# Gated layers of a fused sequence kernel: feed-forward pieces spread over the four steps of a group, the next group's transposes two steps earlier, rotation sums emitted ahead of the softmax's normalisation

## The chip, the cores and the metric

The kernel runs on one core of a Trainium2 chip. The metric is device time in microseconds of one execution; lower is better. TensorE (PE in the profile, PEld for its weight loads) multiplies matrices into PSUM, VectorE (DVE) and ScalarE (ACT) take results out of PSUM and do elementwise work, GpSimd (POOL) works between buffers in SBUF, and SyncE (SP) issues the DMAs.

## What is computed

A sequence of 2 x 2048 tokens with 256 features goes through four blocks, each with a residual connection: a windowed attention layer with a feed-forward, two gated layers (DEPTH is 2), a gated attention unit, and a ternary linear layer. The change concerns the two gated layers alone. Cut to what matters:

```
def _layer(x, wqkv, qs, ksc, wo, lg, lb, w1, b1, w2, b2):
    h = shift_token(x)            # second half of the features comes from the token before
    q, k, v = split(h @ wqkv)     # 8 heads of 64
    q = l2norm(q) * qs
    k = l2norm(k) * ksc
    q, k = rotary_xpos(q, k)
    o = local_attention(q, k, v)  # a token sees itself and the 128 before it, softmax
    x = x + o @ wo
    h = shift_token(x)
    h = layernorm(h) * lg + lb
    a, g = split(h @ w1 + b1)     # 682 each
    h = a * gelu(g)
    x = x + h @ w2 + b2
    return x
```

## The kernel before

The 4096 tokens are 32 tiles of 128 (NT); four tiles make a group (GT = 4, NG = 8). The residual stream R stays in SBUF for the whole kernel. The kernel runs its blocks one after another; everything is in float32, where one matmul of the source shows as two in the profile.

The gated layers are a software pipeline over steps. A table `steps`, filled by `at(step, what, ...)`, says what a step does. With `s0` as the first step of a layer (the second layer begins GAP = 2 steps after the first layer's last tile), tile t is projected in step s0 + t, its scores are made in s0 + t + 1, its weights transposed in s0 + t + 2 and applied to the values in s0 + t + 3. So one step works on four tiles at once, called p (project), q (scores), a (weights) and o (values) in the loop.

The stages of a tile and their lines:

- `project` (L679): four matmuls of the source (two parts of the features, query and key), and two for the values in `project(2)`. ScalarE copies the result to `raw` (L689), squares it into `sq` (L690), copies the values (L686); GpSimd makes the sine products `u2` (L695, L698).
- `norms`: VectorE sums the squares (L710), GpSimd raises the sums to the power -1/2 (L711, L713), giving `rn`.
- `rotate_mul` and `rotate_add`: VectorE's cosine product (L718), the sum with the sine product (L722), and for the key the product with `rn` (L724). `to_features` transposes the result on TensorE (L731) and ScalarE copies it (L733).
- `scores`, in two halves: 32 small matmuls each (L748), mask and row maximum on VectorE (L757), the shift of the exponent (L764). `exponents` is four exps on ScalarE (L775). `normalise` is a reciprocal (L783) and four products (L786) on VectorE.
- `weights_to_keys` transposes a half of the softmax weights (L795, L803); the copies out of PSUM are L799 (ScalarE, first half), L797 (VectorE, second half) and L806 (ScalarE).
- `values` (L820, L832), copies L840 and L841, then `output`: four matmuls with wo (L847) and the sum into R on VectorE (L850).

The feed-forward works on a whole group and is cut into pieces. In the step `prepare`, DMAs fetch the shifted rows `sh` from R, VectorE makes the statistics (L881 to L883), GpSimd rs (L93, L95), VectorE normalises into `h` (L887); `to_features` transposes it (L117, ScalarE L122) and adds b2 to R on GpSimd (L895). Then six `hidden` pieces: four matmuls of the source with 512 columns (L908) for the first five, two (L917) for the sixth, which holds the last 42 features of both halves; gelu on ScalarE (L921) and the product with the other half on VectorE (L922), into one buffer `hh`. Then four `output` pieces, six matmuls each (L929), with a sum into R (L933). Each output piece reads all six parts of `hh`.

`begin` transposes the residual stream of a group before its first projection (L653, copies by ScalarE L654) and carries one column over from the group before (L649, GpSimd). `tables` loads the rotary tables of a group and multiplies them by a scale on GpSimd (L637).

A step has three places where feed-forward pieces stand between its other work, `fill[0]`, `fill[1]`, `fill[2]`. The loop emits a step in a fixed order; what matters of it is: values and scores(0); projection of query and key between exponents(0) and scores(1); norms, rotate_mul(0), project(2); exponents(1) and normalise(0); fill[0]; output; rotate_add(0); both halves of weights_to_keys; rotation of the key; normalise(1); fill[1]; the feed-forward's normalise; transposes of the query; fill[2]; transposes of the key; the feed-forward's to_features; begin.

A tile framework orders the instructions of each engine's queue from this program, with the emitted order as priority, so that a queue's order is near the emitted one but not the same. It also places buffers: all PSUM banks come from one pool of eight (`ps`), `za` and `zb` of `begin` have two buffers, `h`, `hT` and `hh` one.

Of the kernel before, what the change touches and what calls it, by code (L numbers as in the profile page):

```python
# [21 lines left out]
GT = 4  # L22
# [23 lines left out]
def kernel(ctx: ExitStack, tc: tile.TileContext, I: dict, out: bass.AP):  # L46
# [86 lines left out]
    def load_qkv(l):  # L133
        w = {}
        w["wqkv"] = T(wB, [P, KC, 3 * BIN], "wqkvB")
        load(w["wqkv"], I["L0_ffn_wqkv"][l].rearrange("(k p) n -> p k n", p=P))
        return w

    def load_wo(l):
        w = {}  # L140
        w["wo"] = T(wB, [P, BIN // P, D], "woB")
        load(w["wo"], I["L0_ffn_wo"][l].rearrange("(k p) n -> p k n", p=P))
        return w
# [33 lines left out]
    with ExitStack() as st_a:  # L177
# [284 lines left out]
        def at(step, what, *args):  # L462
            steps.setdefault(step, {}).setdefault(what, []).append(args)
# [5 lines left out]
        for g in range(NG):  # L469
            at(GT * g - 2, "load", g)  # L470
            at(GT * g - 1, "begin", g)
            s = GT * (g + 1) + 2
# [7 lines left out]
        groups, tiles, ffns, done = {0: first_group}, {}, {}, None  # L480
        for s in range(min(steps), max(steps) + 1):
            todo = steps.get(s, {})
            p = a = f = n = q = None
# [5 lines left out]
            if "project" in todo:  # L489
                (t,) = todo["project"][0]  # L490
                p = tiles[t] = TileA(t, groups[t // GT])
            if "scores" in todo:
                q = tiles[todo["scores"][0][0]]
            if "attend" in todo:
                a = tiles[todo["attend"][0][0]]
            fill = [lambda x=x: ffns[x[0]].output(x[1]) for x in todo.get("outputs", ())]
            fill += [lambda x=x: ffns[x[0]].hidden(x[1]) for x in todo.get("hidden", ())]
            fill = {0: [], 2: [fill[0:1], fill[1:], []], 4: [fill[0:2], fill[2:3], fill[3:4]]}[len(fill)]
            fill = fill or [[], [], []]
# [58 lines left out]
    def load_weights_c():  # L558
        load(uvw, uvT)
        load(uvb_r, bcast_rows(uvb[0 : 2 * CE], 2 * CE))  # L560

        hs = CS // 2
        load(uvw_sw[:, :, 0:hs], uvT[:, :, 2 * CE + hs : CUV])
        load(uvw_sw[:, :, hs:CS], uvT[:, :, 2 * CE : 2 * CE + hs])

        def column(src):
            return src.rearrange("(p o) -> p o", o=1)

        vectors = [uvb[2 * CE : CUV]]
        vectors += [I["L1_attn_gamma"][i] for i in range(2)] + [I["L1_attn_beta"][i] for i in range(2)]  # L570
        for i, v in enumerate(vectors):
            load(cvec[:, 0, i : i + 1], column(v))
            load(cvec[0:hs, 1, i : i + 1], column(v[hs:CS]))
            load(cvec[hs:CS, 1, i : i + 1], column(v[0:hs]))
        load(lnC[:, 0, :], I["L1_attn_ln_w"].rearrange("(k p) -> p k", p=P))
        load(lnC[:, 1, :], I["L1_attn_ln_b"].rearrange("(k p) -> p k", p=P))
        load(owC, I["o_wT"].rearrange("(k p) n -> p k n", p=P))
        load(obC, bcast_rows(I["L1_attn_o_b"], D))
        load(wD, I["ffn_wT"].rearrange("(k p) n -> p k n", p=P))
        load(bD, bcast_rows(I["L1_ffn_bias"], D))  # L580
        load(alpha, bcast_rows(I["L1_ffn_alpha"], 1))


    with ExitStack() as st_b:
# [47 lines left out]
        def load_tab(g, sv):  # L632

            tab = T(wb, [P, 4, GT, BHD], "tab")
            t0 = g % GPS * GT
            load(tab, I["rope_b"][:, :, t0 : t0 + GT, :])
            nc.gpsimd.tensor_mul(tab, tab, sv.unsqueeze(2).to_broadcast([P, 4, GT, BHD]))  # L637
            return tab

        def begin_b(g, zb_last):  # L640
            seq_start = g % GPS == 0
            Rg = R[:, g * GT : (g + 1) * GT, :]

            za = T(wb, [P, GN], "za")
            zb = T(wb, [P, GN + 1], "zb")
            if seq_start:
                nc.gpsimd.memset(zb[:, 0:1], 0.0)
            else:
                nc.gpsimd.tensor_copy(zb[:, 0:1], zb_last[:, GN : GN + 1])  # L649
            for k, dst in enumerate((za, zb[:, 1 : GN + 1])):  # L650
                pt = bank4()
                for tt in range(GT):
                    nc.tensor.transpose(pt[:, tt, :], Rg[:, tt, k * P : (k + 1) * P], ident)  # L653
                nc.scalar.copy(dst, pt.rearrange("p t c -> p (t c)"))  # L654
            return za, zb
# [287 lines left out]
        for l in range(BL):  # L943
            s0 = l * (NT + GAP)
            for t in range(NT):
                at(s0 + t, "project", l, t)
                at(s0 + t + 1, "scores", l, t)
                at(s0 + t + 2, "weights", l, t)
                at(s0 + t + 3, "values", l, t)
                if t % GT == 0:  # L950
                    at(s0 + t - 2, "tables", l, t // GT)
                    at(s0 + t - 1, "begin", l, t // GT)
            for g in range(NG):
                s = s0 + GT * (g + 1) + 3
                at(s, "prepare", l, g)
                for c in range(BNC):
                    at(s + 1 + c // 3, "hidden", l, g, c)
                for tt in range(GT):
                    at(s + 3 + tt // 2, "outputs", l, g, tt)
            at(s0 + NT - 1, "free_qkv", l)  # L960
            at(s0 + NT + 2, "free_wo", l)
            at(s0 + NT + 7, "free_ffn", l)
# [4 lines left out]
        groups, tiles, ffns = {}, {}, {}  # L967
        sh = None
        for s in range(min(steps), max(steps) + 1):
            todo = steps.get(s, {})  # L970
            p = a = q = o = None
            if "project" in todo:
                l, t = todo["project"][0]
                if l == BL - 1 and t == GT:
                    load_weights_c()
                p = tiles[l, t] = Tile(l, t, wts[l], tabs[l, t // GT], *groups[l, t // GT], tiles.get((l, t - 1)))
            if "scores" in todo:
                q = tiles[todo["scores"][0]]
            if "weights" in todo:
                a = tiles[todo["weights"][0]]  # L980
            if "values" in todo:
                o = tiles[todo["values"][0]]
            fill = [lambda x=x: ffns[x[0], x[1]].output(x[2]) for x in todo.get("outputs", ())]
            fill += [lambda x=x: ffns[x[0], x[1]].hidden(x[2]) for x in todo.get("hidden", ())]
            for l, g in todo.get("tables", ()):
                tabs[l, g] = load_tab(g, scales[l])
            if "prepare" in todo:
                l, g = todo["prepare"][0]
                f = ffns[l, g] = Ffn(l, g, wts[l])
                sh = f.shifted(sh)  # L990
            fill += [lambda: None] * (3 - len(fill))

            if o:
                o.values()
                o.prev = None
            if a:
                a.swap_values()
            if q:
                q.scores(0)
            if p:  # L1000
                p.project(0)
            if q:
                q.exponents(0)
            if p:
                p.project(1)
            if q:
                q.scores(1)
            if p:
                p.norms()
                p.rotate_mul(0)  # L1010
                p.project(2)
            if q:
                q.exponents(1)
                q.normalise(0)
            fill[0]()
            if o:
                o.output()
                tiles.pop((o.l, o.t - 1), None)
            if p:
                p.rotate_add(0)  # L1020
            if a:
                a.weights_to_keys(0)
                a.weights_to_keys(1)
            if p:
                p.rotate_mul(1)
                p.rotate_add(1)
            if q:
                q.normalise(1)
            fill[1]()
            if "prepare" in todo:  # L1030
                f.normalise()
            if p:
                p.to_features(0)
            fill[2]()
            if p:
                p.to_features(1)
            if "prepare" in todo:
                f.to_features()
            for l, g in todo.get("begin", ()):
                groups[l, g] = begin_b(g, groups[l, g - 1][1] if g else None)  # L1040
            for (l,) in todo.get("free_qkv", ()):
                if l + 1 < BL:
                    wts[l + 1] = load_qkv(l + 1)
            for (l,) in todo.get("free_wo", ()):
                if l + 1 < BL:
                    wts[l + 1].update(load_wo(l + 1))
            for (l,) in todo.get("free_ffn", ()):
                if l + 1 < BL:
                    wts[l + 1].update(load_ffn(l + 1))
# [303 lines left out]
```

## Time and profile before

| what | value |
|---|---|
| runs, us | 3016.64, 3003.9, 3003.57 |
| median, us | 3003.9 |
| profiled execution, us | 3012.32 |
| its span, first to last instruction, us | 3010.5 |
| mean granted TensorE clock | 0.959 |

The profile is one execution. Its page gives the busy time of every engine; a trace of it can be asked for a window, an engine or a line. In a timeline, a line is: start in us, duration in us, engine, source line, operation, what it writes and reads, shapes, how many were merged, and in brackets the idle time ahead of it with what is taken to have ended it. In sums by stage, a line is: window, its length, then for PE, PEld, DVE, ACT and POOL the busy time with the number of instructions, then the granted clock as a share of full speed, the DMA share and GB/s.

The costliest lines of the gated layers on TensorE, from the groups by line:

| line | what | instructions | busy, us |
|---|---|---|---|
| L908 | hidden pieces | 640 | 287.4 |
| L679 | projections, both parts | 768 | 411.7 |
| L929 | output pieces | 768 | 176.3 |
| L847 | attention output | 512 | 121.0 |
| L748 | scores | 4032 | 116.6 |

ScalarE loads a table of functions 28 times ahead of gelu (L921) and 28 times ahead of exp (L775) in these layers, 1283 ns each in the mean.

### The profile page before, as it was taken

What the parts mean: (1) busy time and instruction counts of PE and PEld (TensorE: products, weight loads), DVE (VectorE), ACT (ScalarE), POOL (GpSimd) and SP (SyncE); (2) the same over time, 40 slices, a digit from 0 to 9 for tenths busy, and PEclk for the clock granted to TensorE, in tenths of its full rate; (3) what the DMA queues carried; (4) which work ended last, traced back from release to release, by engine and by line L of the source; (5) the groups of instructions that cost most, each with busy time, mean ns of one, the idle gap of its engine ahead of it and who ended that gap; (6) DMA issues with size and microseconds to landing.
All of it is one profiled execution on the core that took longest, in us unless ns stands there. A gap on an engine that the chain in (4) does not pass through costs nothing. (4 is left out here: it accounts for less than half of the span.)

```text
span 3010.5 us, 50610 instructions
## 1 busy us (share of the span) xinstructions
PE 2727.0 (91%) x20146; PEld 1687.9 (56%) x20146; DVE 1703.0 (57%) x4457; ACT 1148.4 (38%) x2441; POOL 962.4 (32%) x935
## 2 busy tenths in 40 slices
PE   5788888896899999998989999999999999899998
PEld 3455556663566666665656666666544455444454
DVE  6766676634656566665666556665553334643333
ACT  2434443524555555554655555554230000210000
POOL 4443444324433333332344333342410012400001
PEclk8889999997899999999999999999999999999999
DMA  5000000002100100111111100101100000000000
GB/s 153 14 27 25 27 20 20 20 18 67 26 19 19 26 23 22 26 36 34 34 42 29 29 20 26 33 22 26 47 27 0 7 8 7 21 7 4 7 6 13
DMA packets 72764, 78.17 MB, mean 26 GB/s; under 512 B 18686, under 2 KB 57937, under 8 KB 72529
## 3 DMA queue, kind: packets, MB, share of 16 engines
q1 hardware_dynamic: 72528, 74.94, 8.9%
q8 instruction: 159, 2.61, 0.4%
q14 instruction: 77, 0.62, 0.1%
HBM read 42.50 MB, written 8.40 MB: 17 GB/s over the span
## 5 line engine op out<-in xcount | busy, mean ns | idle before, releaser
L1251 PE MATMUL ps<-V,s 128*128 128x512 f32 x1024 | 468.4, 593 | 3.2 <-DVE s L1183 3.2
L775 ACT ACTIVATE S<-S,shift,rn 128x192 f32<-128x192 f32 x512 | 274.3, 538 | 247.6 <-DVE shift L764 247.2
L1251 PEld LDWEIGHTS ps<-V,s 128*128 128x128 f32 x1024 | 190.6, 190 | 226.3 <-issue 220.4
L695 POOL TENSOR_TENSOR u<-raw,tab 128x256 f32<-128x256 f32 x128 | 124.0, 969 | 513.2 <-ACT raw L689 513.2
L908 PE MATMUL ps<-hT,w1B 128*128 128x512 f32 x640 | 287.4, 593 | 0.4 <-ACT hT L122 0.4
L679 PE MATMUL ps<-wqkvB,za 128*128 128x512 f32 x384 | 213.8, 639 | 5.9 <-ACT za L654 5.9
L1206 POOL TENSOR_SCALAR veC<-mvC 128x1 f32<-128x1 f32 x32 | 16.5, 517 | 601.1 <-DVE mvC L1204 601.1
L1179 DVE SCALAR_TENSOR_TENSOR s<-ps,strip 128x512 f32<-128x512 f32 x128 | 88.3, 690 | 206.9 <-PE ps L1173 206.9
L365 POOL TENSOR_TENSOR S<-S,mxA 128x1024 f32<-128x1024 f32 x64 | 121.2, 1894 | 259.2 <-DVE mxA L364 215.2
L679 PE MATMUL ps<-wqkvB,zb 128*128 128x512 f32 x384 | 197.9, 597 | 0.0
L713 POOL TENSOR_TENSOR rn<-ss,mhalf 128x16 f32<-128x16 f32 x64 | 195.5, 3055 | 5.2
L1194 ACT COPY oCT<-ps 128x512 f32<-128x512 f32 x32 | 18.7, 585 | 467.1 <-PE ps L1192 467.1
L908 PEld LDWEIGHTS ps<-hT,w1B 128*128 128x128 f32 x640 | 117.9, 190 | 131.0 <-issue 123.4
L929 PE MATMUL ps<-w2B,hh 128*128 128x256 f32 x768 | 176.3, 381 | 2.4 <-DVE top L757 2.4
L757 DVE CUSTOM_DVE_ANT_0 S<-ps,maskB 128x192 f32<-128x192 f32 x512 | 151.5, 350 | 22.9 <-PE ps L748 22.9
L731 PE MATMUL ps<-ident,u 128*128 128x128 f32 x512 | 80.2, 286 | 92.7 <-DVE rdB L783 57.5
L929 PEld LDWEIGHTS ps<-w2B,hh 128*128 128x128 f32 x768 | 143.8, 190 | 35.7 <-issue 11.5
L786 DVE TENSOR_SCALAR S<-S,rdB 128x192 f32<-128x192 f32 x512 | 159.2, 362 | 2.2
L718 DVE TENSOR_TENSOR u<-raw,tab 128x512 f32<-128x512 f32 x128 | 91.4, 715 | 113.3 <-ACT raw L689 109.7
L439 PE MATMUL ps<-hT,wf 128*128 128x512 f32 x256 | 131.9, 651 | 25.4 <-DVE oT L404 20.1
L722 DVE TENSOR_TENSOR u<-u,u 128x512 f32<-128x512 f32 x128 | 90.0, 703 | 89.6 <-POOL u L698 86.7
L731 PEld LDWEIGHTS ps<-ident,u 128*128 128x128 f32 x512 | 63.8, 147 | 129.7 <-issue 63.2
(210 smaller groups left out, 5566.2 us busy)
## 6 DMA issues: line engine op xcount, KB each, us to landing
vs<-v SPq DMA_DIRECT2D x128, 128.0 KB, 2.4
tab<-in_rope_b_dram SPq DMA_DIRECT2D x16, 512.0 KB, 3.8
xg<-in_L_attn_x_dram SPq DMA_DIRECT2D x8, 512.0 KB
xr<-in_L_attn_x_dram SPq DMA_DIRECT2D x8, 512.0 KB, 7.1
xs<-xr SPq DMA_DIRECT2D x8, 512.0 KB, 2.7
h<-xs SPq DMA_DIRECT2D x8, 512.0 KB, 3.6
rc<-in_rope_c_dram SPq DMA_DIRECT2D x8, 512.0 KB, 4.1
out_dram<-R SPq DMA_DIRECT2D x32, 128.0 KB, 1.7
```

The costliest lines, as they stand in the source:

```text
L365: nc.gpsimd.tensor_sub(Sh, Sh, mc.unsqueeze(2).to_broadcast([P, 2 * AG, P]))
L439: nc.tensor.matmul(pm, wf1[:, k, c * P : (c + 1) * P], self.hT[:, k, :], start=k == 0, stop=k == KC - 1)
L679: nc.tensor.matmul(pm, src[:, cols], self.w["wqkv"][:, k, part * BIN : (part + 1) * BIN], start=k == 0, stop=k == 1,)
L695: nc.gpsimd.tensor_mul(u2[:, :, 0:hd2], x[:, :, hd2:BHD], sin[:, :, 0:hd2].to_broadcast([P, BH, hd2]))
L713: nc.gpsimd.tensor_tensor(self.rn, ss, mhalf, ALU.pow)
L731: nc.tensor.transpose(pt[:, j, :], self.u1[part][:, 2 * j : 2 * j + 2, :], ident)
L757: nc.vector.tensor_tensor_reduce(S[:, e, jj, :], sc[e][:, jj * KW : (jj + 1) * KW], self.mask[:, jj, :], 1.0, -3.0e38, ALU.add, ALU.max, t ...
L775: nc.scalar.activation(S[:, e, jj, :], S[:, e, jj, :], AF.Exp, bias=self.shift[half][:, a : a + 1], scale=self.rn[:, head : head + 1], acc ...
L786: nc.vector.tensor_scalar_mul(S[:, e, jj, :], S[:, e, jj, :], rd[:, a : a + 1])
L908: nc.tensor.matmul(pm, w["w1"][:, k, half, c * P : (c + 1) * P], hT[:, k, :], start=k == 0, stop=k == KC - 1,)
L929: nc.tensor.matmul(pm[:, 0:D], hh[:, c, tt * P : (tt + 1) * P], self.w["w2"][:, c, :], start=c == 0, stop=c == BNC - 1,)
L1251: nc.tensor.matmul(acc[i], s2[:, i * P : (i + 1) * P], self.V[:, J, :], start=J == 0, stop=J == TPS - 1,)
```

## The change

Three things are moved; no operation is added or taken out.

1. The pieces. With s as the step that prepares a group, the six hidden pieces stood in s + 1 (three) and s + 2 (three), the outputs in s + 3 (two) and s + 4 (two), which is the next group's prepare step. Now there are two hidden pieces in each of s + 1, s + 2 and s + 3, one output in s + 3 after them, and three in s + 4. Hidden and output pieces share one list, `fill`, in the order in which `at` put them there. In s + 3 the order is hidden 4, hidden 5, output 0.
2. `begin` of a group moves from the step before the group's first tile, which is a prepare step in the run of a layer, to two steps earlier, which is s + 2.
3. In the loop, `rotate_add(0)` is emitted before `output` and no longer after it, and `normalise(0)` after the key's rotation and no longer before `fill[0]`; `fill[1]` is emitted before `normalise(1)`.

```diff
                 if t % GT == 0:
                     at(s0 + t - 2, "tables", l, t // GT)
-                    at(s0 + t - 1, "begin", l, t // GT)
+                    at(s0 + t - 3, "begin", l, t // GT)
             for g in range(NG):
                 s = s0 + GT * (g + 1) + 3
                 at(s, "prepare", l, g)
                 for c in range(BNC):
-                    at(s + 1 + c // 3, "hidden", l, g, c)
+                    at(s + 1 + c // 2, "fill", l, g, "hidden", c)
                 for tt in range(GT):
-                    at(s + 3 + tt // 2, "outputs", l, g, tt)
+                    at(s + 3 + (tt + 2) // 3, "fill", l, g, "output", tt)
...
-            fill = [lambda x=x: ffns[x[0], x[1]].output(x[2]) for x in todo.get("outputs", ())]
-            fill += [lambda x=x: ffns[x[0], x[1]].hidden(x[2]) for x in todo.get("hidden", ())]
+            fill = [lambda x=x: getattr(ffns[x[0], x[1]], x[2])(x[3]) for x in todo.get("fill", ())]
...
             if q:
                 q.exponents(1)
-                q.normalise(0)
             fill[0]()
+            if p:
+                p.rotate_add(0)
             if o:
                 o.output()
                 tiles.pop((o.l, o.t - 1), None)
-            if p:
-                p.rotate_add(0)
             if a:
                 a.weights_to_keys(0)
                 a.weights_to_keys(1)
...
                 p.rotate_mul(1)
                 p.rotate_add(1)
             if q:
+                q.normalise(0)
+            fill[1]()
+            if q:
                 q.normalise(1)
-            fill[1]()
             if "prepare" in todo:
                 f.normalise()
```

## The prediction

> **What bounds the kernel now.** I read the page's head first, then the sums by stage over the gated layers, then the timelines of TensorE, VectorE and ScalarE through one group of four steps, then the granted clock.
>
> ```profile
> span 3010.5 us, 50610 instructions
> PE 2727.0 (91%) x20146; PEld 1687.9 (56%) x20146; DVE 1703.0 (57%) x4457; ACT 1148.4 (38%) x2441; POOL 962.4 (32%) x935
> ```
>
> TensorE is the busy engine. The changed loop runs from about 672 to 2160 us. The sums by stage for four consecutive steps, each cut at the first projection matmul (time, then busy time of PE, PEld, DVE, ACT, POOL, clock, DMA):
>
> ```profile
> 1096.89:1119.86 22.97, 22.97 (x201) 13.36 (x193) 13.37 (x41) 12.82 (x30) 6.72 (x6) 1.00 0.06 13
> 1119.86:1141.11 21.25, 21.25 (x195) 12.60 (x189) 12.72 (x41) 13.87 (x31) 6.63 (x6) 1.00 0.06 14
> 1141.11:1158.95 17.84, 17.84 (x198) 13.40 (x193) 10.30 (x37) 10.77 (x27) 6.63 (x6) 1.00 0.13 31
> 1158.95:1188.16 29.21, 22.07 (x214) 16.44 (x209) 19.03 (x59) 11.65 (x30) 13.02 (x11) 0.94 0.10 29
> ```
>
> I call them A, B, C, D; D prepares the group's feed-forward. In A, B, C TensorE is busy all the time: they cannot shrink except by losing work. All idle time is in D, and only there is the clock below 1. So the question is what becomes of D. Its TensorE queue:
>
> ```profile
> 1172.35 0.66 PE L795 MATMUL ps<-ident,S 128*128 128x128 f32 x4 [1.97 <-ACT sq L690]
> 1176.09 0.60 PE L731 MATMUL ps<-ident,u 128*128 128x128 f32 x4
> 1179.38 0.63 PE L731 MATMUL ps<-ident,u 128*128 128x128 f32 x4 [2.69 <-DVE rdB L783]
> 1183.66 0.66 PE L653 MATMUL ps<-ident,R 128*128 128x128 f32 x4 [2.27 <-DVE PT L797]
> ```
>
> Three waits: 1.97 us for a bank that ScalarE empties late; 2.69 us between the query's and the key's transposes; 2.27 us for a bank behind VectorE's copy L797. The releaser named for the second is an accident of neighbours: the key's transposes read what L724 writes, and L724 ends at 1179.2. VectorE and ScalarE say why all three are late:
>
> ```profile
> 1160.01 0.29 DVE L882 BATCH_NORM_STATS2 st<-sh 128x6 f32<-128x128 f32 x1 [3.06 <-DMA sh<-R]
> 1163.34 0.35 DVE L887 TENSOR_SCALAR h<-R,mv,rs 128x128 f32<-128x128 f32 x1 [1.48 <-POOL rs L95]
> 1165.72 0.35 DVE L757 CUSTOM_DVE_ANT_0 S<-ps,maskB 128x192 f32<-128x192 f32 x1
> ...
> 1178.55 0.69 DVE L724 TENSOR_TENSOR u<-u,rn 128x512 f32<-128x512 f32 x1 [1.07 <-POOL rn L713]
> ...
> 1180.16 2.65 DVE L786 TENSOR_SCALAR S<-S,rdB 128x192 f32<-128x192 f32 x2
> ```
>
> ```profile
> 1168.14 0.55 ACT L775 ACTIVATE S<-S,shift,rn 128x192 f32<-128x192 f32 x1 [9.33 <-DVE shift L764]
> ```
>
> The scores were in PSUM at 1159.0, but VectorE's queue has the feed-forward's normalisation ahead of them. It waits for the shifted rows and for rs, and L757 begins 6.7 us late. Everything behind it (exponents, the projections' copies, the key's norm, L724) is late by as much. [...]
>
> ```profile
> 1176.60:1179.45 2.85, 0.16 (x2) 0.10 (x2) 1.75 (x5) 2.13 (x7) 1.91 (x1) 1.00 0.51 165
> 1184.20:1188.20 4.00, 4.00 (x99) 3.74 (x97) 0.42 (x1) 0.96 (x2) 0.18 (x1) 0.57 0.03 6
> ```
>
> [...] here the groups of such loads show a mean of 1283 ns. [...] here two L786 took 2.65 us beside a GpSimd product of 2.45 us (L637), against 0.54 us for two at 1001.33.
>
> **The change, part by part.** Start-to-start times on TensorE at full clock: a hidden piece 3.44 us (1217.40 to 1220.84), the short sixth 1.72 (1227.75 to 1229.47), an output piece 2.59 (1147.38 to 1149.97), eight transposes 0.94 (1179.85 to 1180.79). A step without pieces is 12.65: 22.97 − 3 × 3.44, and equally 21.25 − 8.60 and 17.84 − 5.18.
>
> *Pieces.* Nothing is added. A has two hidden instead of three: 12.65 + 6.88 = 19.5. B has two and takes begin's transposes: 12.65 + 6.88 + 0.94 = 20.5. C has a hidden, the short one and one output: 12.65 + 3.44 + 1.72 + 2.59 = 20.4. D has three outputs and no begin: 12.65 + 7.77 + 0.94 = 21.4. Sum 81.8, as before; what changes is only the loss above it. Before, five cycles in the first layer took 447.9 us (828.86 to 1276.77), five in the second 443.9, so 89.2 a cycle: 7.4 us lost, 5.1 of it idle and 2.3 a slow clock (the busy time, 840.5 / 10 = 84.1, less 81.8).
>
> *The third output in D* stands in the third slot, between the query's and the key's transposes, which was empty in D. Its 2.59 us take the place of the 2.69 us wait[...]. Steps without any piece (idle 2.9 us each near 755 to 790) have the same gap there; A, B and C, with two pieces, had none.
>
> *Gelu in C.* ScalarE gets a load before gelu in C and one before exp in D: two more a cycle, 2 × 1.28 us. That in C is hidden, as A's and B's are. That in D is not: in today's C, which follows a step with gelu, the load starts right after shift (1142.70), ahead of the first exponent and so of the projections' copies. Price: +1.28 us on D's chain. What works against it: between the last tile's L850, which releases the shifted rows' DMA, and D's scores, TensorE gets the short piece and an output, 4.3 us, where there was one output of 2.6. In B, whose fill resembles the new C, L850 ends 2.96 us before the next step's first matmul (1227.03 to 1229.99); in C it was 0.9 (1155.67 to 1156.57). The new C is 0.85 us shorter than B (20.4 against 21.25), which leaves 2.1, so D's wait for rows shrinks by about 1.2. The bounds of this are 0, if L850 stays where it was, and −3.06, the whole wait. I take −1.2 against +1.28: D's chain stays where it is relative to TensorE. So the first wait stays near its usual 1.0 (0.8 to 2.1 over twelve groups), the second falls to some 0.3, the third keeps its mean of 1.1 (12.8 us over twelve groups), since L797 stays behind the softmax and the GpSimd product. Add 0.6 for the clock: 3.0 lost in place of 7.4.
>
> *The short piece before output 0 in C.* That output's last two matmuls need the sixth gate product (L922). TensorE has the query's transposes and ten matmuls between, some 2.6 us; gelu and L922 are 0.68 + 0.75 plus starts, 1.7. Hidden, unless something stands in front of L922.
>
> *begin in B* moves eight transposes, two ScalarE copies of 0.59 and a tiny GpSimd copy, no DMA. The two banks come at the step's end, where A to C never waited; 0 is taken, 0 to 1 us a cycle possible. D is rid of them.
>
> *rotate_add ahead of normalise* changes nothing in amount. VectorE's queue already had L722 ahead of the first normalisation (1171.27 against 1171.88), so the emitted order isn't the queue's order. I take 0; from −0.8 (one L783 and one L786 out of the way of the second scores) to +0.8.
>
> Gain a cycle: 7.4 − 3.0 = 4.4 us. Twelve groups have the full pattern (six in each layer: the first of a layer has no earlier outputs, the last lies at the layer's end): 53 us. I take off 8 for begin's banks and the ends of the layers: **45 us**. The profiled execution took 3012.3, its span 3010.5, so the same kernel profiled would be at about 2967. The median of the runs is 3003.9, 8 us under the profiled one; the difference is taken from it: **2959 us**.
>
> **Rivals.** *The chain is what counts.* D's load costs its 1.28 and the rows come no earlier. The first wait is 2.3, the third 1.5, the clock 1.5: 5.3 lost, 2.1 gained, 25 us in all: 2979. For it: ScalarE's load does sit behind shift in today's C. Against: TensorE's extra work in C.
>
> *The planner keeps its order.* Queue order differs from the emitted one; if the third output lands behind the key's transposes, the 2.7 us pause and slow clock remain, and nothing is gained: 3004. Against: TensorE's queue in D follows the emitted order piece by piece.
>
> *Slower: the rows' wait gets in front of the sixth gate product in C.* VectorE's L882 already stood ahead of an L933 (1160.01, 1160.22), so its position is just about there. The rows land some 22 us into C, output 0 needs L922 at 19.6: a stall of 3.3 plus 2.5 of slow clock, and D still loses 5.0 by its load, L797 and clock. That is 10.8 against 7.4: +3.4 a cycle, +41 us: 3045. It decides once C loses more than 2.4. Against: L922 is ready at about the moment L882 is, and it is emitted first.
>
> **How the numbers follow.** Forecast 0.58, smaller gain 0.22, no effect 0.06, slower 0.14. The 80% range is 2932 to 3000; its low end is a third wait that goes too and the taken-off 8 not needed. Resolution is about 0.5%, 15 us. Faster by more than that: nearly all of the first case and most of the second, 0.74; within 0.11; slower 0.15.
>
> **What would show it.** A, B, C at 19.5, 20.5, 20.4 without idle time, D near 24; 2.59 us of L929 between two groups of L731 in D; 42 loads of each kind in place of 28; hardly any half clock in the loop. It is wrong if C shows idle time before an L929, B before L653, or if D's first wait grows past 2.5 us.

## The result, and the profile after

| | before | changed |
|---|---|---|
| median of the runs, us | 3005.31 (4 runs, 3003.57 to 3016.64) | 3033.45 (4 runs, 3030.71 to 3034.9) |
| profiled execution and its span, us | 3012.32, 3010.5 | 3030.71, 3028.9 |
| mean granted clock | 0.959 | 0.962 |

The ratio on record is 1.0085, 95% interval 1.0058 to 1.0111: the change makes the kernel slower, by 25 us by that ratio and by 28 us from median to median, where 45 us faster was forecast. The page of the changed kernel, its head and two of its groups (busy time, mean ns of one, idle time of the engine ahead of it):

```profile
span 3028.9 us, 50649 instructions
...
PE 2734.7 (90%) x20146; PEld 1684.1 (56%) x20146; DVE 1715.6 (57%) x4457; ACT 1179.0 (39%) x2467; POOL 989.4 (33%) x935
...
L929 PE MATMUL ps<-w2B,hh 128*128 128x256 f32 x768 | 182.1, 383 | 16.5 <-DVE hh L922 15.4
...
L724 DVE TENSOR_TENSOR u<-u,rn 128x512 f32<-128x512 f32 x64 | 67.7, 1058 | 187.0 <-POOL rn L713 187.0
```

The same two groups before:

```profile
L929 PE MATMUL ps<-w2B,hh 128*128 128x256 f32 x768 | 176.3, 381 | 2.4 <-DVE top L757 2.4
L724 DVE TENSOR_TENSOR u<-u,rn 128x512 f32<-128x512 f32 x64 | 46.4, 725 | 95.0 <-POOL rn L713 95.0
```

TensorE does the same 20146 matmuls. It now waits 16.5 us ahead of output pieces, 15.4 of it for the gate product, where it waited 2.4 before. L724, the key's product with `rn`, takes 1058 ns in the mean where the median of before is 692, and VectorE idles 187 us ahead of it, about twice as long as before. The sums by stage, four steps cut as before:

```profile
1099.34:1118.87 19.53, 19.53 (x192) 11.88 (x185) 12.42 (x40) 12.04 (x29) 7.47 (x6) 1.00 0.07 16
1118.87:1139.71 20.84, 20.62 (x199) 12.73 (x193) 12.17 (x40) 14.29 (x32) 6.88 (x6) 1.00 0.06 14
1139.71:1161.88 22.17, 20.94 (x199) 13.19 (x193) 13.05 (x47) 13.19 (x30) 6.99 (x7) 1.00 0.11 25
1161.88:1190.71 28.83, 24.68 (x218) 18.88 (x213) 17.18 (x51) 12.09 (x29) 13.36 (x11) 0.88 0.11 29
```

A has the forecast length. B and C now have idle time, 0.22 and 1.23 us, where they had none. D did not shrink to 24: it has 4.15 us idle and a clock of 0.88. TensorE's queue at the end of C and in D:

```profile
1156.72 0.70 PE L929 MATMUL ps<-w2B,hh 128*128 128x256 f32 x2 [0.21 <-DVE hh L922]
1158.43 0.70 PE L929 MATMUL ps<-w2B,hh 128*128 128x256 f32 x2 [1.01 <-DVE hh L922]
...
1177.17 0.60 PE L731 MATMUL ps<-ident,u 128*128 128x128 f32 x4
1177.61 2.76 PE L929 MATMUL ps<-w2B,hh 128*128 128x256 f32 x12
1183.25 0.66 PE L731 MATMUL ps<-ident,u 128*128 128x128 f32 x4 [2.89 <-DVE R L933]
```

The third output stands where it was meant to, between the two groups of L731, and TensorE still waits 2.89 us behind it (2.69 before, with nothing in between). The releaser named is again a neighbour; the matmuls read what L724 writes, and L724 ends at 1182.86. VectorE shows why, first in C, then in D:

```profile
1149.43 0.68 DVE L722 TENSOR_TENSOR u<-u,u 128x512 f32<-128x512 f32 x1
...
1153.26 0.69 DVE L724 TENSOR_TENSOR u<-u,rn 128x512 f32<-128x512 f32 x1 [3.07 <-POOL rn L713]
1153.87 1.00 DVE L786 TENSOR_SCALAR S<-S,rdB 128x192 f32<-128x192 f32 x4
...
1155.00 1.01 DVE L786 TENSOR_SCALAR S<-S,rdB 128x192 f32<-128x192 f32 x4
1155.92 0.74 DVE L922 SCALAR_TENSOR_TENSOR hh<-ps,b1B,gl 128x512 f32<-128x512 f32 x1
...
1157.62 0.75 DVE L922 SCALAR_TENSOR_TENSOR hh<-ps,b1B,gl 42x512 f32<-42x512 f32 x1
1160.16 0.49 DVE L882 BATCH_NORM_STATS2 st<-sh 128x6 f32<-128x128 f32 x2 [1.79 <-DMA sh<-R]
...
1180.04 2.82 DVE L724 TENSOR_TENSOR u<-u,rn 128x512 f32<-128x512 f32 x1 [3.08 <-POOL rn L713]
```

In B, C and D all eight softmax products of the step (L786) now stand behind L724; before, four of them stood ahead of it. VectorE has nothing to do for 3 us while GpSimd makes `rn`, and then has 2 us of products ahead of the gate product that output 0 waits for. In D, L724 itself takes 2.82 us. GpSimd in that D:

```profile
1177.08 2.93 POOL L713 TENSOR_TENSOR rn<-ss,mhalf 128x16 f32<-128x16 f32 x1
1179.98 2.34 POOL L637 TENSOR_TENSOR tab<-tab,sv 128x1024 f32<-128x1024 f32 x1
```

The table's product L637 starts as `rn` is done, 0.06 us ahead of L724, which ends 0.54 us after it. Of the 64 executions of L724, 11 take over 2.8 us; before, one did.

### The profile page after: what moved, and what is told of

Same layout as the page of the kernel before. It is cut to its first block, busy times and chain, and to the rows that moved or that the text cites. A ratio compares the mean times of both kernels' runs of the same rounds, so it can differ in the third digit from the quotient of the medians.

```text
span 3028.9 us, 50649 instructions
## 1 busy us (share of the span) xinstructions
PE 2734.7 (90%) x20146; PEld 1684.1 (56%) x20146; DVE 1715.6 (57%) x4457; ACT 1179.0 (39%) x2467; POOL 989.4 (33%) x935
## 5 line engine op out<-in xcount | busy, mean ns | idle before, releaser
L713 POOL TENSOR_TENSOR rn<-ss,mhalf 128x16 f32<-128x16 f32 x64 | 197.5, 3085 | 5.3
L929 PE MATMUL ps<-w2B,hh 128*128 128x256 f32 x768 | 182.1, 383 | 16.5 <-DVE hh L922 15.4
L724 DVE TENSOR_TENSOR u<-u,rn 128x512 f32<-128x512 f32 x64 | 67.7, 1058 | 187.0 <-POOL rn L713 187.0
L718 DVE TENSOR_TENSOR u<-raw,tab 128x512 f32<-128x512 f32 x128 | 97.9, 766 | 125.5 <-ACT raw L689 124.4
L731 PE MATMUL ps<-ident,u 128*128 128x128 f32 x512 | 82.5, 290 | 95.7 <-DVE u L724 52.8
L733 ACT COPY qkT<-ps 128x512 f32<-128x512 f32 x128 | 73.7, 584 | 201.7 <-PE ps L731 201.7
L786 DVE TENSOR_SCALAR S<-S,rdB 128x192 f32<-128x192 f32 x512 | 143.9, 334 | 2.4
```

The source lines that it names most:

```text
L713: nc.gpsimd.tensor_tensor(self.rn, ss, mhalf, ALU.pow)
L718: nc.vector.tensor_mul(u1, self.raw[:, part], cos.to_broadcast([P, BH, BHD]))
L786: nc.vector.tensor_scalar_mul(S[:, e, jj, :], S[:, e, jj, :], rd[:, a : a + 1])
L929: nc.tensor.matmul(pm[:, 0:D], hh[:, c, tt * P : (tt + 1) * P], self.w["w2"][:, c, :], start=c == 0, stop=c == BNC - 1,)
```

## The experiments

Two theories of the loss stood against each other. ORDER: edit 3 costs the time: the planner, given `normalise(0)` behind the key's rotation, leaves VectorE without work ahead of L724 and with 2 us of it behind. PORT: the table's product and L724 meet in D, where L724 takes 2.82 us instead of 0.69, and that costs it. All times are medians, in us, and ratios are to the kernel before, measured beside them (3005.94 in the first four experiments, 3006.35 in the others).

**old_order**: the changed kernel with the emitted order of before, so the pieces and `begin` moved alone.

```diff
                 q.exponents(1)
+                q.normalise(0)
             fill[0]()
-            if p:
-                p.rotate_add(0)
             if o:
                 o.output()
...
+            if p:
+                p.rotate_add(0)
...
             if q:
-                q.normalise(0)
-            fill[1]()
-            if q:
                 q.normalise(1)
+            fill[1]()
```

> The changed kernel with the emitted order of before (normalise(0) ahead of the first piece, rotate_add(0) behind output); pieces and begin stay moved. Theory ORDER: normalise(0), emitted behind the key's rotation, now stands in VectorE's queue behind L724, which waits 3.1 us for rn, so the gate products and the copies behind it are 1 us later; C loses 1.2 us and D 0.65 us by it, 12 groups: 22 us faster than the changed kernel, about 3011, C without idle time. Theory PORT: GpSimd's table product L637 begins at the moment at which L724 does and makes it 2.8 us instead of 0.7; its place is the same here, so L724 stays at 2.8 us in D and the time stays within 5 us of 3033.

Measured: 2971.7 (2969.03 to 2974.71), ratio 0.9881 [0.9866, 0.9895]. The moved pieces are 34 us faster than before; edit 3 on top of them costs 62 us, where ORDER had put 22 on it. VectorE's queue in C and in D:

```profile
1049.30 0.99 DVE L786 TENSOR_SCALAR S<-S,rdB 128x192 f32<-128x192 f32 x4
...
1052.88 0.69 DVE L724 TENSOR_TENSOR u<-u,rn 128x512 f32<-128x512 f32 x1 [1.90 <-POOL rn L713]
1053.49 1.00 DVE L786 TENSOR_SCALAR S<-S,rdB 128x192 f32<-128x192 f32 x4
1054.41 0.74 DVE L922 SCALAR_TENSOR_TENSOR hh<-ps,b1B,gl 128x512 f32<-128x512 f32 x1
...
1078.81 2.83 DVE L724 TENSOR_TENSOR u<-u,rn 128x512 f32<-128x512 f32 x1 [1.80 <-POOL rn L713]
```

With half of the products ahead of L724, VectorE's pause is 1.90 instead of 3.07, and L922 starts 1.53 us after L724 does instead of 2.66. C is 20.78 long with 0.11 idle. The 2.83 in D is there too (10 of 64 L724 are this long here), with L637 on GpSimd from 1078.75, so the meeting of the two does not come from edit 3 but from the moved pieces.

**only_order**: the kernel before with edit 3 alone (the reverse of that diff, on before).

> The kernel before with the new emitted order alone; pieces and begin as before. Theory ORDER: L724 is in front of normalise(0) here too, but C holds only output pieces, whose matmuls wait for no product of the same step, so C stays without idle time; D may lose up to 1 us a group by later copies: 3005 to 3017. Theory PORT: D has no load of the exp table in front and L710 ahead of the key's L718, so L637 begins after L724: no lengthened L724, 3005 within 5 us.

Measured: 3069.88 (3066.45 to 3071.11), ratio 1.0204 [1.019, 1.0219]. Edit 3 costs 64 us without the moved pieces as well, so it is not a matter of where the pieces stand. Both theories had put it at 3017 or less, and C, expected without idle time, is 1.54 us longer (table below). Steps without any piece show the way to `rn` by itself; here is one of only_order, VectorE and GpSimd in order of time, and then the same step of the kernel before:

```profile
779.98 0.68 DVE L718 TENSOR_TENSOR u<-raw,tab 128x512 f32<-128x512 f32 x1
...
780.08 0.69 POOL L711 TENSOR_SCALAR ss<-ss 128x16 f32<-128x16 f32 x1 [1.74 <-DVE shift L764]
...
780.81 0.68 DVE L722 TENSOR_TENSOR u<-u,u 128x512 f32<-128x512 f32 x1
780.85 3.42 POOL L713 TENSOR_TENSOR rn<-ss,mhalf 128x16 f32<-128x16 f32 x1
```

```profile
780.88 0.77 DVE L786 TENSOR_SCALAR S<-S,rdB 128x192 f32<-128x192 f32 x3
...
780.97 0.32 POOL L711 TENSOR_SCALAR ss<-ss 128x16 f32<-128x16 f32 x1 [1.74 <-DVE shift L764]
...
781.38 3.06 POOL L713 TENSOR_TENSOR rn<-ss,mhalf 128x16 f32<-128x16 f32 x1
```

Before, L711 takes 0.32 us and L713 3.06, and three products L786 start 0.09 us ahead of L711; now the cosine product L718 starts 0.10 us ahead of L711, which takes 0.69, and the rotation sum L722 0.04 us ahead of L713, which takes 3.42. From L711's start to `rn`'s end it takes 4.19 us here (780.08 to 784.27) instead of 3.47 (780.97 to 784.44). In these steps the later `rn` is the whole of the added idle time: in the mean of four of them, from the start of L710 to the end of `rn` it takes 5.50 us in only_order and in the changed kernel, 4.75 before and in old_order, and TensorE idles 3.65 to 3.67 us a step instead of 2.91 to 2.95. In B and C `rn` comes only 0.25 us later by edit 3 (table below).

**port_free**: the changed kernel with the table's product on VectorE.

```diff
-            nc.gpsimd.tensor_mul(tab, tab, sv.unsqueeze(2).to_broadcast([P, 4, GT, BHD]))
+            nc.vector.tensor_mul(tab, tab, sv.unsqueeze(2).to_broadcast([P, 4, GT, BHD]))
```

> The changed kernel with the table product L637 on VectorE instead of GpSimd, nothing else. Theory PORT: L724 in D is 0.7 us again, the pause ahead of the key's transposes falls from 2.9 to below 1 us and with it most of the slow clock: 2.1 us and up to 1.7 us of slow clock in 12 groups, 25 to 45 us faster, 2988 to 3008. Theory ORDER: the pause is made by the wait for rn and by the later normalisation, so the time stays within 8 us of 3033.

Measured: 3001.43 (2995.5 to 3009.72), ratio 0.9982 [0.9971, 0.9993]: 32 us off the changed kernel. No L724 takes over 694 ns, and D falls from 27.65 to 24.94 us in the mean, by 1.3 us of idle time and 1.4 us of TensorE busy time for the same matmuls. The granted clock is 0.88 in the D of the changed kernel shown, with 24.68 us busy, and 0.93 in the same D here, with 23.42. PORT is right on its size, but it is not the whole. The run takes all of the table's product off GpSimd, and VectorE has 1.2 us more to do, so the 32 us are what the move is worth, not the price of the two meeting in D alone; L724 itself is 1.9 us shorter in the mean of the D's.

**both_mended**: old_order and port_free together.

> Pieces and begin moved as in the changed kernel, emitted order of before, table product L637 on VectorE. If PORT and ORDER both hold and add, the gains add: 22 + 25 to 45 us off 3033, 2966 to 2986, faster than the kernel before, which is what the prediction forecast for the moved pieces. If the load of the exp table in D (1.28 us on the chain) or the moved begin is the cause instead, the time stays above 3010.

Measured: 2937.25 (2936.35 to 2940.88), ratio 0.9768 [0.9754, 0.9782]. The two single gains, 61.8 and 32.0 from 3033.45, sum to 2939.7: they add. That it is below the expected 2966 to 2986 is ORDER's 22, which was 62. The load of the exp table in D and the moved begin are still there, so neither is what made the changed kernel slow: for that the time was to stay above 3010. TensorE and VectorE in a D, in order of time:

```profile
1150.08 2.76 PE L929 MATMUL ps<-w2B,hh 128*128 128x256 f32 x12
...
1152.49 0.69 DVE L724 TENSOR_TENSOR u<-u,rn 128x512 f32<-128x512 f32 x1 [1.80 <-POOL rn L713]
...
1153.23 0.66 PE L731 MATMUL ps<-ident,u 128*128 128x128 f32 x4 [0.40 <-DVE u L724]
...
1154.95 1.21 DVE L637 TENSOR_TENSOR tab<-tab,sv 128x1024 f32<-128x1024 f32 x1
```

The wait behind the third output is 0.40 us: now the output fills the gap. The sum by stage of this step,

```profile
1134.31:1157.66 23.35, 22.12 (x219) 16.51 (x213) 16.06 (x52) 11.97 (x29) 11.05 (x10) 1.00 0.13 35
```

has the clock at 1.00, and 2.56 us less TensorE time than the D of the changed kernel at 0.88, for the same work.

**only_fill**: old_order with `begin` where it was (`t - 1`), so that the pieces alone are moved.

> Pieces moved alone: begin where it was before, emitted order of before. Theory that the pieces bring the gain: D holds begin's 0.94 us again and B loses it, the sum is equal, and the pause ahead of the key's transposes is where it was in old_order: 2966 to 2982. Theory that begin's move brings the gain (D rid of begin's banks): above 2990.

Measured: 2970.44 (2968.56 to 2977.3), ratio 0.9885 [0.9862, 0.9908]. It cannot be told from old_order: `begin`'s move is worth nothing that these runs show. B is 19.53 instead of 20.26 without it and D 26.30 instead of 25.41.

**before_table_on_dve**: the kernel before with the edit of port_free.

> The kernel before with the table product L637 on VectorE, nothing else. Theory PORT holds before the change too, with L786 as the victim (2.65 us for two against 0.54): the third wait in D goes in the groups that show it, 1 to 1.5 us in twelve groups with some slow clock, 2985 to 2998. If the collision is without effect there, 3006 within 5 us.

Measured: 2993.22 (2989.14 to 2995.78), ratio 0.9953 [0.9937, 0.997]: 13 us. The table's product on GpSimd cost 13 us before, where two L786 beside it took 2.65 us for 0.54, and costs 32 to 34 with the pieces moved, where L724 takes 2.82 for 0.69. What the moved pieces are worth without it is 2993.22 less 2937.25, 56 us.

**both_mended_max_on_dve** and **changed_max_on_dve**: the small GpSimd instruction L711 moved to VectorE, in both_mended and in the changed kernel.

```diff
-                nc.gpsimd.tensor_scalar_max(ss, ss, 1e-24)
+                nc.vector.tensor_scalar_max(ss, ss, 1e-24)
```

> As both_mended, and the small maximum L711 ahead of the power moved from GpSimd to VectorE, which takes one change of engine and 0.25 us of GpSimd out of the chain to rn. The key's transposes in D still wait 0.5 us: up to 0.5 us in 13 groups and in the steps without pieces, 2925 to 2938. If the chain to rn no longer matters, 2937 within 4 us.

> The changed kernel with L711 on VectorE. In the changed kernel L711 stands beside VectorE's L722 and takes 0.62 us against 0.25 to 0.32 before. If this longer chain to rn is a large part of what normalise(0) costs, the steps without pieces fall from 3.65 us idle to below 3.0 and the time by 15 us or more, to below 3018. If the cost lies in the products queued behind L724 alone, 3033 to 3023.

Measured: 2934.94 (2933.15 to 2938.23), ratio 0.9761 [0.9739, 0.9783], no more than both_mended by what can be told; and 3001.4 (2998.73 to 3004.45), ratio 0.9984 [0.9977, 0.9992], 32 us off the changed kernel, below the 3018 that was to speak for the way to `rn`. The number alone doesn't decide it, because the edit did two things. In the steps without pieces `rn` does come sooner, 4.95 us after L710's start instead of 5.50, and TensorE's idle time falls from 3.67 to 3.11 (below 3.0 was expected): there the way to `rn` is what costs. In C and D `rn` comes no earlier in the step (13.55 and 18.38 us for 13.52 and 18.27 in the changed kernel). What differs there is that one L786 came to stand ahead of L724, and that L850 starts 0.2 us earlier in C and 0.6 in D, with D 1.2 us shorter. That fits the products behind L724 as the cost in C and D, but doesn't separate it further.

**Where edit 3's time lies.** The means of the four steps over the inner groups of both layers (twelve of A, B and C, ten of D):

| | A | B | C | D | sum |
|---|---|---|---|---|---|
| before | 23.04 | 21.25 | 17.84 | 27.03 | 89.2 |
| forecast | 19.5 | 20.5 | 20.4 | 24.4 | 84.8 |
| changed | 19.77 | 20.73 | 22.16 | 27.65 | 90.3 |
| old_order | 19.56 | 20.26 | 20.78 | 25.41 | 86.0 |
| only_order | 22.97 | 21.74 | 19.38 | 29.14 | 93.2 |
| port_free | 20.11 | 20.73 | 22.16 | 24.94 | 87.9 |
| both_mended | 19.56 | 20.26 | 20.78 | 23.29 | 83.9 |

Edit 3 adds 4.1 us to a cycle (before to only_order) or 4.3 (old_order to changed); twelve cycles make 49 to 52 of its 62 to 64 us, and most of the rest lies in the first eight steps of each layer (3.0 and 2.9 us in the first layer; 8.0 and 7.7 in the second, where the first layer's last pieces stand among them). Within a step, old_order against the changed kernel, means of the same steps in us after the first projection matmul:

| | A | B | C | D |
|---|---|---|---|---|
| L786 ahead of L724 | 4, 3 | 4, 0 | 4, 0 | 4, 0 |
| `rn` ends | 12.82, 13.32 | 13.26, 13.52 | 13.27, 13.52 | 18.04, 18.27 |
| L850 starts | 15.25, 15.98 | 15.48, 16.87 | 15.49, 16.87 | 20.81, 22.21 |
| L797 starts | 15.91, 16.64 | 16.14, 17.53 | 15.82, 17.20 | 21.83, 23.41 |
| TensorE's L820 starts | 17.16, 17.35 | 17.88, 18.32 | 18.40, 19.79 | 22.63, 24.17 |

In B, C and D the four products more behind L724 make everything that follows on VectorE 1.4 to 1.6 us late, of which a later `rn` is 0.25. In C and D TensorE is late by just that at L820, which reads the copy L797; in C the whole step is 1.38 longer. B has some slack and loses 0.47. A, where three products stay ahead of L724, is late mostly by `rn` (0.50 of 0.73) and loses 0.2. D is 2.24 longer: 1.15 us of idle time, and 1.09 of busy time for the same matmuls; the granted clock is 0.88 in the D of the changed kernel shown and 1.00 in the same D of old_order.

## Why the prediction was wrong

**The step that failed** is "rotate_add ahead of normalise changes nothing in amount ... I take 0; from −0.8 ... to +0.8". It costs 62 us beside the moved pieces and 64 without them, 4 us a cycle where at most 0.8 was allowed for. I looked at what was emitted and at one pair of the queue, L722 of the query and the first L783, and not at what the late `normalise(0)` would leave between L710 and L724. That was the place to look. In the D of before that the prediction shows, VectorE had three L786, the key's cosine product and rotation sum and a residual sum there, and TensorE's second wait in D was already read as L724's:

```profile
1173.76 1.21 DVE L710 TENSOR_REDUCE ss<-sq 128x16 f32<-128x1024 f32 x1
...
1174.96 0.77 DVE L786 TENSOR_SCALAR S<-S,rdB 128x192 f32<-128x192 f32 x3
```

Of edit 3 only the move of `normalise(0)` counts. With `normalise(0)` late and the other two calls put back, every engine's queue is instruction for instruction that of the changed kernel; with `normalise(0)` early and the other two moved, it is that of old_order (a reading of the built queues; neither was run). Between old_order and the changed kernel TensorE's and SyncE's queues are the same; VectorE's differs in 780 of 4906 places, GpSimd's in 10 and ScalarE's in 8.

What the runs show in its place: the products come behind L724, and L724 waits for GpSimd's 3 us. VectorE idles through that time, and L922, L850 and L797 follow the products, 1.4 us late, with TensorE behind them in C and D. A slower way to `rn` is in the traces too: it is a fifth of the delay in B, C and D, most of it in A, and the whole of it in the steps without pieces.

**The second wait failed next.** It was put at 0.3 us and is 2.9 in nine of the ten D's. "The GpSimd product" stood in the third wait, kept at 1.1 us, with L786 as the victim. In the changed kernel L637 meets L724 instead. Its start is set by the table's DMA, which can go once the key's cosine product L718 has read the old table: it was issued at 1176.42 before, behind an L718 of 1175.65, and at 1175.14 after, behind one of 1174.23 that stands ahead of L710. Before, L637 then started only 1.73 us after `rn`; now it starts as `rn` ends. First the DMA's issue and L637 before, then the issue after:

```profile
1176.42 0.60 SPq L56 DMA_DIRECT2D tab<-in_rope_b_dram  x1
1180.24 2.45 POOL L637 TENSOR_TENSOR tab<-tab,sv 128x1024 f32<-128x1024 f32 x1 [1.73 <-DVE R L850]
1175.14 0.60 SPq L56 DMA_DIRECT2D tab<-in_rope_b_dram  x1
```

The releaser named, L850, doesn't touch the table; that L637 waited for the DMA is inferred from the issue and from the 3.8 us that such a DMA takes to land by the page of before. With port_free the second wait is 0.75, so 2.1 of the 2.9 us went with the table's product on GpSimd. That costs 32 us and is the larger part of why "its 2.59 us take the place of the 2.69 us wait" did not hold: TensorE comes later to the same place, and L724 is later by as much. With both causes removed the wait is 0.40, so the reasoning on the third output was right and its neighbour was missed.

**The slow clock** was put at 0.6 us a cycle, which was the author's estimate. In the ten D's of the changed kernel TensorE is busy for 22.15 and 22.16 us in the two with a granted clock of 1.00, for 23.32 to 23.50 in the five with 0.94, and for 24.68 or 24.69 in the three with 0.88: 1.4 us over 22.15 in the mean. In the D's of old_order it is 0.4 us over 22.15. In the D that the prediction shows, the clock stands at 0.50 from 1184.67 to 1188.08, after waits of 1.97, 2.69 and 2.27 us; in the D of the changed kernel shown, from 1183.81 to 1190.63, after the wait of 2.89. In both_mended it is 1.00 in the D shown, where the two longest waits are 0.64 and 0.40. The second wait alone doesn't decide it: another D of the changed kernel (982.39 to 1008.95) has one of 2.87 and a clock of 1.00. What brings the clock down isn't shown beyond that.

**The short piece before output 0** was called "hidden, unless something stands in front of L922". Something did, the eight L786: 1.22 us in C, about 15 us over twelve cycles. In old_order it was 0.11, all but hidden, as forecast.

**What held.** A, B and C are 19.53, 20.40 and 20.78 in old_order's regular groups against 19.5, 20.5 and 20.4. Loads: 41 of each kind for the 42 forecast, 1283 ns each. D's load of exp stands where it was put, ahead of the first exponent:

```profile
1168.08 1.28 ACT L775 ACT_TABLE_LOAD   x1 [6.34 <-DVE shift L764]
```

The wait for rows is 1.79 us here and was 3.06 in the D shown of before, but that was one of the two longest: the means are 1.90 and 2.22. Measured from D's first projection the rows do come sooner: VectorE begins with them (L882) 1.6 us before it instead of 0.2 after it, 1.8 us earlier where 1.2 was forecast, and the first exponent starts 7.64 us into D instead of 8.37, with the load ahead of it. The first wait of D was 0.75 in the mean (1.0 forecast). That gelu in C costs D nothing more was not tried by itself. The forecast gain of 45 us lies between the 34 measured with the table's product on GpSimd and the 56 measured with it on VectorE in both kernels; that it lies so near is in part luck, since L637 beside L724, which takes the 34 down, was not foreseen.

**The rivals.** "The planner keeps its order" fell: the output is where it was emitted. "The chain is what counts" fell in its premise, since the rows came 1.8 us earlier. The slower rival had the right sign and nearly the time (3045 for 3033), but by luck, for its mechanism did not occur: L882, with its wait for rows, stands behind both L922. The 2.5 us of slow clock in it were the author's estimate; the C shown has a clock of 1.00.

## What to carry to other kernels

Where work is moved later in a queue, ask first which wait it was filling and what stands behind it at its new place: the same amount of VectorE work cost 62 us when half of it moved from ahead of a 3 us GpSimd result to behind it. A forecast for a planned queue needs the planned order between the producer and the consumer of each cross-engine result, not the emitted one. And before a gap is filled, check what sets its end, and whether another engine's instruction that was late by luck can now start together with the critical one (0.06 us apart here, and L724 took 2.82 us for 0.69). The best version here, both_mended with or without the small maximum on VectorE, is 2.3 to 2.4% faster than before and needed both mends.

## What the runs showed of the hardware

A VectorE product of two SBUF tensors (L724) that started 0.06 us after a GpSimd product (L637) took 2.82 us instead of 0.69 and ended 0.54 us after it; moving the GpSimd product to VectorE gained 32 us over the kernel, and no L724 took over 0.694 us there. In only_order the VectorE product started first: L718 at 779.98, L711 on GpSimd 0.10 us later, and L711 ended only 0.11 us after L718. That is long for L711, on 16 columns: it took 0.25 us at the least before and in old_order, and 0.62 to 0.70 in the changed kernel (medians 256 ns in old_order, 626 in the changed kernel). The power L713 took 3.42 us where VectorE's L722 started 0.04 us ahead of it, and 3.06 in the same step before (2.93 in the D shown). On VectorE the table's product was shorter too: 1.21 us instead of 2.34.
